# Numerators and denominators from one pass of 32x32 tiles, gathered by SBUF transfers

## The chip, the cores and the metric

The kernel runs on one core of a Trainium2 chip. The metric is the device time of one execution in microseconds (us). TensorE (PE) multiplies matrices and writes into PSUM; its weight loads are a row of their own in the profile (PEld). VectorE (DVE) and ScalarE (ACT) read and write PSUM and SBUF, GpSimd (POOL) here works on SBUF, and SyncE (SP) issues most DMA transfers. Each engine works through its own queue in order and waits where a semaphore says so.

## The reference

The input x has 16 images of 256 channels and 28x28 pixels. After a group norm, two layers follow that replace a 3x3 convolution by a lookup. Each channel has 16 centroids of 9 values. A pixel's 3x3 patch in a channel is compared with the channel's centroids, a softmax over the 16 distances gives weights, and the weights select rows of a table:

```python
d = sum(p*p) - 2*einsum('bncs,cks->bnck', p, centroids) + sum(centroids*centroids)
attn = softmax(-d, axis=-1)
lut = einsum('cks,cso->cko', centroids, w_sub)
out = einsum('bnck,cko->bno', attn, lut)
```

Batch norm and relu follow layer 1; batch norm, a squeeze-and-excite gate, two residual additions and a relu follow layer 2. The kernel never forms `lut`. It forms, per channel and pixel, the softmax-weighted centroid (9 numerators over one denominator) and multiplies this by `w_sub`. All data are float32.

## The kernel before

**Blocks.** An image of one layer is worked in four blocks: `hh` is the half of the 256 channels, `t` the upper or lower 14 rows, N = 14 x 28 = 392 pixels. There are 2 x 16 x 4 = 128 blocks (`blocks`, in the order `BLOCKS`). A block goes through these steps.

1. `patches` loads two tiles `pt` with the shifted rows of 128 channels from a copy in DRAM: 12 DMAs per block on SP.
2. `logits` (L622) multiplies them with the centroids in four passes, `mm` = 0 to 3. A pass is 16 matmuls with weights of 32x32; they fill the 16 squares of the array, and each streams 392 columns. In the profile every float32 matmul shows as two, so a pass is 32 records. A pass fills two tiles of two PSUM banks.
3. `exps` turns the logits into exponentials `e` in SBUF with two ACT instructions a pass. In layer 2 the pass `mm` = 0 of the blocks with `hh` = 0 goes through `wide_copy` to `wide_exp` instead (ACT, DVE, POOL, DVE, ACT), which subtracts the largest of the 16 logits first.
4. `num_a` (L673) multiplies `e` with eight of the nine centroid values: 8 matmuls of 64x32 per `mm`. `num_b` (L686) multiplies it with the ninth and with ones: 16 matmuls of 128x32 in one group. The ninth numerators and the denominators come out in different rows of one pair of banks. `split_r`, `join_r`, `split_q` and `join_q` (two on ACT, two on DVE) sort them into a tile `r` of denominators and a tile `qo` of ninth numerators.
5. `recip_dve` inverts `r`. `spread` copies it with stream shuffles to the rows where each numerator stands (`rb`, on DVE). `scale_a` multiplies the numerators by it on the way out of PSUM, on DVE. One or two pairs per block go another way: `copy_a` on ACT takes them out of PSUM, and `scale_q` on POOL multiplies them, as it does `qo`.

**Products.** The four blocks of an image are multiplied with the halves of `w_sub` by a scheme that needs seven products in place of eight (`PRODUCTS`: A11, S1, S3, S2, S4, A12, A22). Between them `mix` subtracts one block's tiles from another's, on POOL, in place (four times five instructions per image). A product is nine *stacks*: for each of nine k, two matmuls of 128x64 weights over 392 columns, accumulated in one bank. `acc_copy` (ACT) and `acc_add` (DVE) take the results out, and `reg_add` (POOL) adds two regions.

**Order.** The order of all work is written out by hand: `at(cluster, sub, function, ...)` puts a call at a place of a grid, and the calls are issued in the order of their places. There are two clusters per block. A product is one run of nine stacks behind one pass, except that S1 is split into seven and two. Which banks a step takes is set by `ROLES` and, for the first blocks, by `EARLY`; the ring has four tags of two banks. Numerators live in 12 tiles `qp` of two k each and 4 tiles `qo`.

**Around it.** While an image of layer 1 is worked, the next image's group norm is computed, written to DRAM (`to_home1`), and the finished image is written to DRAM for layer 2 (`to_home2`, an indirect DMA issued by POOL). While an image of layer 2 is worked, the previous one is gated, added and stored (`finish_...`, `store`). Some steps during layer 1 sort the codes and weights of layer 2 (`prep_...`, `sums_...`).

## Time and profile before

| | |
|---|---|
| median of 3 runs | 2579.1 us (2579.03 to 2579.27) |
| the profiled execution | 2580.25 us |
| its span, first to last instruction | 2578.8 us |
| granted TensorE clock | 1.000 |
| busy: PE, DVE, ACT, POOL | 99%, 69%, 53%, 74% of the span |
| moved by DMA | 372.09 MB |

A group row of the profile reads: line, engine, operation, output <- inputs, shapes, how many; then busy time in us, mean ns of one, idle time of the engine just before them and what ended it. A row of the order in time reads: start, duration, engine, line, operation. Layer 1 covers roughly the first half of the span. A long PE run between two weight-load rows can be read from their starts, since every matmul group begins with its loads.

### The profile page before, as it was taken

How to read it: one execution, taken by the hardware profiler on the slowest of the kernel's cores; microseconds unless marked ns; L12 is line 12 of the kernel's file. 1: busy time of each engine (PE TensorE's matmuls, PEld its weight loads, DVE VectorE, ACT ScalarE, POOL GpSimd, SP SyncE). 2: the span in 40 equal slices, each digit the busy share in tenths (PEclk: the TensorE clock that was granted, in tenths of full speed). 3: DMA queues.
4: the chain of work that ended last, by engine and by line, in shares of the span. 5: the costliest groups of instructions: out<-in, count | busy, mean ns of one | idle time of the engine just before them, and what ended most of it. 6: DMA issues, size and time to landing. Idle time of an engine off the chain costs nothing.

```text
span 2578.8 us, 85941 instructions
## 1 busy us (share of the span) xinstructions
PE 2561.5 (99%) x37082; PEld 1027.1 (40%) x37082; DVE 1776.3 (69%) x3797; ACT 1372.6 (53%) x1913; POOL 1911.6 (74%) x1346
## 2 busy tenths in 40 slices
PE   8999999999999999999999999999999999999998
PEld 3343334433343333433334334344444344433434
DVE  8766656666667666566676767767776667767676
ACT  6444444444444445444455655555655655555665
POOL 7686666776668776667676887878878788787786
PEclk9999999999999999999999999999999999999999
DMA  7556656565545575664664444444445444444442
GB/s 234 167 130 184 199 169 189 161 170 172 164 143 148 158 197 174 169 173 134 178 171 104 109 115 128 120 120 122 104 126 129 119 117 113 118 125 130 118 106 66
DMA packets 213289, 372.09 MB, mean 144 GB/s; under 512 B 29496, under 2 KB 183528, under 8 KB 212328
## 3 DMA queue, kind: packets, MB, share of 16 engines
q1 hardware_dynamic: 206584, 333.75, 48.2%
q0 software_dynamic: 6176, 32.66, 3.5%
q8 instruction: 296, 4.85, 0.8%
q14 instruction: 89, 0.73, 0.1%
q10 hardware_dynamic: 144, 0.10, 0.0%
HBM read 288.46 MB, written 77.95 MB: 142 GB/s over the span
## 4 chain that ended last, share of the span: by engine, by line
PE 96%; POOL 1%; DVE 1%; ACT 1%; DMA 1%; issue 0%; SPq 0%; POOLq 0%; DVEq 0%; ACTq 0%
PE acc L756 51%; PE lg L622 17%; PE na L673 14%; PE nb L686 13%; POOL qp L765 0%; ACT e L633 0%; DMA pt<-home 0%; ACT pt L1143 0%; POOL qp L736 0%; DVE qp L747 0%; DMA xt<-in_x 0%; POOL qo L763 0%; DMA d_sc<-score_t 0%; SPq L600 0%; PE sep L1049 0%
## 5 line engine op out<-in xcount | busy, mean ns | idle before, releaser
L756 PE MATMUL acc<-qp,wall 128*64 128x392 f32 x6176 | 1088.1, 494 | 1.0 <-POOL qp L765 0.4
L633 ACT ACTIVATE e<-lg 128x784 f32<-128x784 f32 x960 | 738.1, 821 | 624.7 <-PE lg L622 622.8
L765 POOL TENSOR_TENSOR qp<-qp,qp 128x784 f32<-128x784 f32 x512 | 946.3, 1872 | 146.2 <-DVE qp L747 145.7
L756 PEld LDWEIGHTS acc<-qp,wall 128*64 128x64 f32 x6176 | 424.3, 137 | 626.4 <-issue 529.8
L728 DVE STREAM_SHUFFLE rb<-r 128x392 f32<-128x392 f32 x1024 | 553.6, 608 | 0.0
L622 PE MATMUL lg<-pt,wd 32*32 32x392 f32 x15872 | 469.0, 499 | 0.6 <-DMA pt<-home 0.3
L699 DVE SCALAR_TENSOR_TENSOR r<-nb,kst,r 128x392 f32<-128x392 f32 x128 | 80.0, 625 | 432.7 <-ACT r L695 428.7
L673 PE MATMUL na<-e,cwa 64*32 64x392 f32 x8192 | 374.2, 492 | 0.0
L747 DVE TENSOR_TENSOR qp<-na,rb 128x784 f32<-128x784 f32 x352 | 333.9, 972 | 57.7 <-PE na L673 45.2
L686 PE MATMUL nb<-e,cwb 128*32 128x392 f32 x4096 | 366.3, 495 | 0.2 <-ACT e L633 0.2
L736 POOL TENSOR_TENSOR qo<-qo,rb 128x392 f32<-128x392 f32 x128 | 132.9, 1038 | 283.9 <-DVE rb L724 283.9
L713 DVE RECIPROCAL r<-r 128x392 f32<-128x392 f32 x128 | 333.2, 2603 | 4.4
L736 POOL TENSOR_TENSOR qp<-qp,rb 128x784 f32<-128x784 f32 x160 | 296.7, 1864 | 2.8
L673 PEld LDWEIGHTS na<-e,cwa 64*32 64x32 f32 x8192 | 182.4, 106 | 182.9 <-issue 73.0
L622 PEld LDWEIGHTS lg<-pt,wd 32*32 32x32 f32 x15872 | 116.1, 103 | 277.0 <-issue 235.6
L686 PEld LDWEIGHTS nb<-e,cwb 128*32 128x32 f32 x4096 | 135.0, 109 | 222.9 <-issue 155.0
L756 PE MATMUL acc<-qp,w_A 128*64 128x392 f32 x1024 | 181.1, 495 | 0.0
L695 ACT ACTIVATE r<-nb,kst 128x392 f32<-128x392 f32 x128 | 86.8, 678 | 154.9 <-PE nb L686 151.8
L756 PE MATMUL acc<-qo,wall 128*64 128x392 f32 (+1 forms) x772 | 159.2, 491 | 0.0
L657 POOL TENSOR_TENSOR z<-z,mx 128x1568 f32<-128x1568 f32 x32 | 91.9, 2872 | 86.1 <-DVE mx L651 84.8
L741 ACT COPY qp<-na 128x784 f32<-128x784 f32 x160 | 130.1, 813 | 21.6 <-PE na L673 20.1
L763 POOL TENSOR_TENSOR qo<-qo,qo 128x392 f32<-128x392 f32 x128 | 131.6, 1028 | 0.1
(244 smaller groups left out, 1624.4 us busy)
## 6 DMA issues: line engine op xcount, KB each, us to landing
pt<-home SPq DMA_DIRECT2D x744, 209.0 KB
pt<-home SPq DMA_DIRECT2D x744, 104.5 KB
home<-xpad SPq DMA_DIRECT2D x30, 899.0 KB
xt<-in_x SPq DMA_DIRECT2D x30, 784.0 KB
out_dram<-y SPq DMA_DIRECT2D x31, 392.0 KB
pt<-in_p SPq DMA_DIRECT2D x6, 784.0 KB
d_wS<-st SPq DMA_DIRECT2D x12, 192.0 KB
wall<-d_wS SPq DMA_DIRECT2D x4, 576.0 KB
```

The source lines that it names most:

```text
L622: nc.tensor.matmul(bk[32 * c : 32 * c + 32, :N].rearrange("p (r w) -> p r w", w=W), lhsT=(wx[u["hh"]] if early(u) else wts["wd", u["hh"]]) ...
L633: nc.scalar.activation(eg[:, 2 * i : 2 * i + 2, :], bk[:, :, :N], AF.Exp, scale=2.0)
L673: nc.tensor.matmul(bs[32 * i : 32 * i + 32, r, :N], lhsT=wts["cwa", u["hh"]][64 * r : 64 * r + 64, mm, i, :], rhs=es[64 * r : 64 * r + 64, ...
L686: nc.tensor.matmul(bs[32 * i : 32 * i + 32, mm >> 1, :N], lhsT=wts["cwb", u["hh"]][:, mm, i, :], rhs=es[:, i, :], start=mm % 2 == 0, stop= ...
L713: nc.vector.reciprocal(u["r"], u["r"])
L728: nc.vector.stream_shuffle(rb[:, r, :], u["r"], mask_of(2 * mm + r))
L736: nc.gpsimd.tensor_tensor(q, q, u.pop(("rb", mm)), ALU.mult)
L741: nc.scalar.copy(pair(u, mm), u.pop(("na", mm))[:, :, :N])
L747: nc.vector.tensor_mul(pair(u, mm), u.pop(("na", mm))[:, :, :N], rb)
L756: nc.tensor.matmul(accs[key][o : o + AW, : cols[1] - cols[0]], lhsT=wl[w][:, k, o : o + AW], rhs=us["q", k][:, cols[0] : cols[1]], start=f ...
L763: nc.gpsimd.tensor_tensor(out_u["q", 8], in0["q", 8], in1["q", 8], ALU.subtract)
L765: nc.gpsimd.tensor_tensor(pair(out_u, mm), pair(in0, mm), pair(in1, mm), ALU.subtract)
```

## The change

Steps 4 and 5 and the order are replaced.

- `codes` takes the place of `num_a` and `num_b`: per `mm` one pass of 16 matmuls with weights of 32x32, like `logits`, gives the eight numerators, the ninth numerator and the denominator of 64 channels together, in two tiles of two banks (`cd`).
- `take` copies each `cd` to SBUF with two instructions on ACT (in block 0 one of them on DVE). For `mm` 1 and 3 the copy goes into a tile `qq` of four k; for `mm` 2 and 0 it goes into a tile `g`.
- `moves` issues DMAs from SBUF to SBUF on SP: for each `mm` one of 32 rows of 392 numbers into the denominators `sum` and one into the ninth numerators `qo`, and for `mm` 2 and 0 one more of 64 rows of 1568 numbers from `g` into the other rows of `qq`. That is ten per block.
- `recip` sums `sum` (for a later test) and inverts it on DVE. `spread` is as before, without the shuffle for the ninth numerator. `scale` multiplies in SBUF: three pairs per block on DVE, one pair and the ninth numerator on POOL.
- Every pass, `logits` or `codes`, is followed by two stacks: the order is now counted in positions, eight to a block and 32 to an image, and the stacks of the seven products are laid out evenly over the positions.
- PSUM is three rotating tags of two banks for passes and two single banks for products.
- The preparation of layer 2's codes gives one array `cn` in place of `cwa` and `cwb`, and the weights are loaded by two DMAs with every second row in place of one. At the end `gate_wide` and `finish_wide` are gone, and the image before the last is finished by `finish_fast`.

```diff
-NQ = {"pair": 12, "one": 4}
+NQ = {"quad": 9, "one": 5}
+PRODUCTS = (("A11", 0), ("S1", 0), ("S4", 2), ("S3", 1), ("S2", 0), ("A12", 3), ("A22", 0))
+NPOS = {1: 5, 2: 7, 3: 9, 0: 11}
+IMG, START = 32, 24
+HEAD = ((18, 24), (25, 31), (32, 37.7))
...
+    def banks(name, tag=None):
+        if tag is None:
+            spin[0] = (spin[0] + 1) % 3
+            tag = spin[0] - 1 if spin[0] else 2
+        return p_ring.tile([P, 2, 512], F32, tag=f"t{tag}", name=name)
...
+    def codes(u, mm):
+        bs = [banks("cd") for _ in range(2)]
+        es = u.pop(("e", mm))
+        for c in range(4):
+            for i in range(4):
                 nc.tensor.matmul(
+                    bs[c // 2][32 * i : 32 * i + 32, c % 2, :N],
+                    lhsT=wts["cn", u["hh"]][32 * c : 32 * c + 32, mm, i, :], rhs=es[32 * c : 32 * c + 32, i, :],
                     start=True, stop=True,
                 )
...
+    def take(u, mm, engines):
+        x, guest = divmod(turn_of(mm), 2)
+        t = epool.tile([P, 4, N], F32, tag="g", name="g", bufs=2) if guest else quad(u, x)
+        for n, bk in enumerate(u.pop(("cd", mm))):
+            if engines[n] is nc.scalar:
+                nc.scalar.copy(t[:, 2 * n : 2 * n + 2, :], bk[:, :, :N])
...
+    def moves(u, mm, eng=None):
+        eng = eng or nc.sync
+        turn, t = turn_of(mm), u.pop(("cd", mm))
+        guest = turn & 1
+        for off, dst in ((1 - guest, u["s"]), (3 - guest, lone(u))):
+            eng.dma_start(dst[turn::4, :], t[off::16])
+        if guest:
+            eng.dma_start(quad(u, turn >> 1)[1::2], t[1::2])
+
+    def recip(u):
+        w = u["w"]
+        nc.vector.tensor_reduce(wsum[:, w : w + 1], u["s"], axis=AX.X, op=ALU.add)
+        nc.vector.reciprocal(u["s"], u["s"])
...
+    def scale(u, x, eng):
+        if x == 4:
+            eng.tensor_tensor(lone(u), lone(u), u["s"], ALU.mult)
         else:
+            eng.tensor_tensor(pair(u, x), pair(u, x), u.pop(("rb", x)), ALU.mult)
...
+        for mm in range(4):
+            at(g + 2 * mm, logits, u, mm)
...
+            s = g + NPOS[mm]
+            at(s, codes, u, mm)
+            at(s + 0.1, take, u, mm, (nc.scalar, nc.vector if j == 0 else nc.scalar))
+            at(s + 0.12, moves, u, mm)
+        s = g + 13.2
+        at(s, recip, u)
+        at(s + 1.3, scale, u, 4, nc.gpsimd)
+        for i, d in enumerate(SPREADS):
+            at(s + 1.35 + 0.9 * i, spread, u, d)
+            at(s + 1.4 + 0.9 * i, scale, u, d, nc.gpsimd if d == 3 else nc.vector)
...
+            for k in range(NS):
+                pos = x0 + (x1 - x0) * (k + 0.5) / NS
+                pos = int(pos) + 0.2 + 0.75 * (pos - int(pos))
+                at(pos, product, (n, w), us[r], w, (k,), k == 0, k == NS - 1, ps=q % 2)
```

## The prediction

> **What bounds the kernel now.** I read the page's sums and its chain of waits first, then the busy time by stretches of both layers, then TensorE's weight loads in order of time, because their starts show what each segment of the PE queue costs.

> ```profile
> span 2578.8 us, 85941 instructions
> PE 2561.5 (99%) x37082; PEld 1027.1 (40%) x37082; DVE 1776.3 (69%) x3797; ACT 1372.6 (53%) x1913; POOL 1911.6 (74%) x1346
> PE 96%; POOL 1%; DVE 1%; ACT 1%; DMA 1%; issue 0%; SPq 0%; POOLq 0%; DVEq 0%; ACTq 0%
> q1 hardware_dynamic: 206584, 333.75, 48.2%
> ```
> ```profile
> 1300.00:2500.00 1200.00, 1199.95 (x17428) 480.19 (x17428) 854.70 (x1688) 697.20 (x967) 946.30 (x573) 1.00 0.46 120
> 400.00:1200.00 800.00, 799.20 (x11642) 317.81 (x11628) 515.82 (x1189) 381.62 (x524) 557.17 (x436) 1.00 0.59 167
> 13.00:40.00 27.00, 25.33 (x466) 10.47 (x468) 22.38 (x61) 17.46 (x25) 22.82 (x34) 1.00 0.83 281
> ```
> The columns of the stretches are PE, PEld, DVE, ACT, POOL busy, granted clock, DMA share, GB/s. PE is busy without a gap in both layers at clock 1.00 and carries 96% of the chain: time is what the PE queue holds, and other engines cost nothing until PE waits for them. The weight loads tell what it holds:

> ```profile
> 1010.09 0.17 PEld L686 LDWEIGHTS nb<-e,cwb 128*32 128x32 f32 x8 [0.64 <-ACT hpad L787]
> ...
> 1012.88 0.23 PEld L622 LDWEIGHTS lg<-pt,wd 32*32 32x32 f32 x32 [0.64 <-issue]
> ...
> 1018.51 0.23 PEld L622 LDWEIGHTS lg<-pt,wd 32*32 32x32 f32 x32 [0.61 <-PE acc L756]
> 1019.38 1.55 PEld L673 LDWEIGHTS na<-e,cwa 64*32 64x32 f32 x48 [0.64 <-issue]
> ...
> 1022.23 0.23 PEld L622 LDWEIGHTS lg<-pt,wd 32*32 32x32 f32 x32 [0.64 <-issue]
> 1023.10 0.20 PEld L756 LDWEIGHTS acc<-qp,wall 128*64 128x64 f32 x4 [0.64 <-issue]
> 1024.57 0.23 PEld L622 LDWEIGHTS lg<-pt,wd 32*32 32x32 f32 x32 [0.61 <-DVE rb L724]
> ...
> 1029.48 0.20 PEld L756 LDWEIGHTS acc<-qp,wall 128*64 128x64 f32 x4 [0.64 <-issue]
> 1035.56 0.23 PEld L622 LDWEIGHTS lg<-pt,wd 32*32 32x32 f32 x32 [0.61 <-issue]
> ```
> Start to next start: a logits pass 0.87 us (1018.51 to 1019.38), na of a block 2.85 (1019.38 to 1022.23), nb 2.79 (1010.09 to 1012.88), a run of two product stacks 1.47 (1023.10 to 1024.57), of nine 6.08 (1029.48 to 1035.56). So a stack is (6.08 - 1.47) / 7 = 0.659 and the change of tile shape adds 1.47 - 2 x 0.659 = 0.15 to a run. An image of one layer is 16 x 0.87 + 4 x 5.64 + 63 x 0.659 + 8 x 0.15 = 79.2; 32 of them are 2534 of the span, and the other 45 are small products, head and tail.

> **The change, term 1: the passes.** Per block na and nb (5.64) go and four passes cd come. cd has lg's tile, 32*32, sixteen matmuls and 392 columns, and stands between stacks as lg does: 0.87, so 3.48. 128 x (3.48 - 5.64) = -276.

> **Term 2: the runs.** The 63 stacks of an image stood in 8 runs (S1 was split); now they stand in 32, two behind each pass. 24 x 0.15 x 32 = +117. Terms 1 and 2: -159, an image of 74.2. A pass and its two stacks, 0.87 + 1.47 = 2.34, are one position of the new order, 32 to an image. [...]

> **Term 3: ScalarE and the PSUM banks.** Each pass, logits and cd alike, must now be copied out by ACT, through three rotating bank pairs.

> ```profile
> 1013.88 1.54 ACT L633 ACTIVATE e<-lg 128x784 f32<-128x784 f32 x2 [0.19 <-PE lg L622]
> ```
> ```profile
> L741 ACT COPY qp<-na 128x784 f32<-128x784 f32 x160 | 130.1, 813 | 21.6 <-PE na L673 20.1
> L705 ACT ACTIVATE qo<-nb,kst 128x392 f32<-128x392 f32 x128 | 87.4, 683 | 0.7 <-DVE r L699 0.7
> L695 ACT ACTIVATE r<-nb,kst 128x392 f32<-128x392 f32 x128 | 86.8, 678 | 154.9 <-PE nb L686 151.8 <-issue 3.1
> L807 ACT ACTIVATE hpad<-hpad,bnsh,bnsc 128x392 f32<-128x392 f32 x64 | 44.2, 719 | 59.8 <-DVE hpad L793 51.8 <-DVE gn_var L570 8.0
> L820 ACT ACTIVATE y<-y,bnsh,bnsc 128x784 f32<-128x784 f32 x30 | 31.0, 1034 | 0.0
> L579 ACT ACTIVATE xpad<-xt,nrm 128x784 f32<-128x784 f32 x30 | 29.7, 1047 | 0.3 <-POOL nrm L573 0.3
> L665 ACT ACTIVATE e<-e 128x1568 f32<-128x1568 f32 x32 | 48.4, 1511 | 72.9 <-DVE e L661 72.9
> ```
> By the stretches ACT has 381.62 / 800 x 79.2 = 37.8 an image in layer 1 and 46.0 in layer 2. Minus the splits (4 x 1.36) and copies (4 or 6 x 0.81), plus 16 x 1.54: 53.7 and 60.3 of 74.2, enough in sum. But a pass at T is taken up from T + 1.00 (1012.88, 1013.88), its first half is free at about T + 1.8, and the pass after next half needs it at T + 2.34, one position later: slack about 0.5. Every other ACT job of 0.7 to 1.5 us makes ACT late; at 1.54 of 2.34 it recovers 0.8 per position. The order puts two to four such jobs on neighbouring positions (layer 1: L807 and L579 near positions 17 to 20; layer 2: gate, norm_both, xn near 18 to 22, and again near 25). I reckon the excess over 0.5 as 1.2 us an image in layer 1 and 2.1 in layer 2: +53. The ends are 0 and all ACT work beside the 32 x 1.54 = 49.3 uncovered, 4.4 and 11.0 an image: 16 x 15.4 = 246. I take a fifth, nearer the lower end, since most of these jobs stand alone on their position and 0.5 + 0.8 swallows them.

> **Term 4: VectorE and GpSimd.** DVE loses the joins, one shuffle and the product out of PSUM, and gets a sum (half of 949) and three products per block with both inputs in SBUF.

> ```profile
> L747 DVE TENSOR_TENSOR qp<-na,rb 128x784 f32<-128x784 f32 x352 | 333.9, 972 | 57.7 <-PE na L673 45.2 <-issue 2.9 <-POOL z L657 0.5
> L699 DVE SCALAR_TENSOR_TENSOR r<-nb,kst,r 128x392 f32<-128x392 f32 x128 | 80.0, 625 | 432.7 <-ACT r L695 428.7
> L724 DVE STREAM_SHUFFLE rb<-r 128x392 f32<-128x392 f32 x128 | 76.6, 598 | 0.0
> L710 DVE SCALAR_TENSOR_TENSOR qo<-nb,kst,qo 128x392 f32<-128x392 f32 x128 | 67.5, 527 | 0.0
> L1131 DVE TENSOR_REDUCE qsum<-qp 128x2 f32<-128x784 f32 x4 | 3.7, 949 | 0.0
> L736 POOL TENSOR_TENSOR qo<-qo,rb 128x392 f32<-128x392 f32 x128 | 132.9, 1038 | 283.9 <-DVE rb L724 283.9
> L736 POOL TENSOR_TENSOR qp<-qp,rb 128x784 f32<-128x784 f32 x160 | 296.7, 1864 | 2.8
> ```
> ```profile
> 67.31 2.73 DVE L239 TENSOR_TENSOR wall<-w_A,wall 128x1152 f32<-128x1152 f32 x1
> ```
> ```profile
> 63.30 5.52 POOL L765 TENSOR_TENSOR qp<-qp,qp 128x784 f32<-128x784 f32 x3 [0.60 <-DVE qp L747]
> 68.78 2.16 POOL L736 TENSOR_TENSOR qo<-qo,rb 128x392 f32<-128x392 f32 x1
> ```
> The one DVE product of two SBUF tensors here waits for POOL's running mix to end at 68.8, and POOL's next takes 2.16 for 1.04: they exclude each other. For 784 columns POOL loses 1.12 x 784 / 1152 = 0.76; DVE takes 0.95 alone and up to 0.95 + 1.86 behind a POOL product, taken 1.6. [...] Per image DVE comes to 51.1 - 19.0 + 1.9 + 12 x 1.6 = 53.2 in layer 1 and 56.4 - 17.0 + 21.1 = 60.5 in layer 2; POOL, with two scales less in layer 2, to 55.2 + 9.1 = 64 and 62.5 - 3.7 + 9.1 = 68. All below 74.2, so nothing in sum; their queues are in order, and late mixes cost the products, which have 1 to 3 positions in hand: +12, with ends 0 and 100.

> **Term 5: the transfers.** Ten more per block on SP, about 1.2 MB.

> ```profile
> L600 SPq DMA_DIRECT2D pt<-home x1488: 543/587/1449, 56.7 to 2515.5; - x186
> DMA to landing us min/median/max: 3.3/5.2/8.3
> ```
> The first row is the time on SP's queue (min, median, max, ns), the second the landing of transfers on the tile home. SP: 22 x 0.587 = 12.9 of 18.6 us per block. Transfers: 154 MB at q1's 48.2% for 333.75 MB is 22 points, 18 us an image; in the shorter image the shares are (0.59 x 79.2 + 18) / 74.2 = 0.87 and 0.73. The moves wait for the copies, and behind them on SP stand the patch loads, whose last issue has about 4 positions, 9.4 us, against a worst landing of 8.3: covered, barely. The sums must land before DVE's reciprocal, 2.2 positions after the last cd: 5.1 - 1.00 - 1.54 - 0.59 = 2.0 us. At 3.3 DVE stands 1.3 a block, with its shuffles, accumulator adds and the turns of the wide blocks behind it: 53 + 5 and 61 + 5 an image, still under 74. Costed in term 4. The preparation of layer 2's codes and weights changes its layout and some transfers; PE's full queue hides it as it does now: 0.

> **Head and tail.** Until position 18 there is no product, and ACT sets the pace: 9 logits and 3 cd at 1.54 and four half cd, 21.6, against 16 x 0.87 + 3 of raw sums on PE. Before, PE was busy 25.33 of 27. +10 (0 to 20). The tail keeps its chain: 0, give or take 5.

> **Sum.** -159 + 53 + 12 + 10 = -84. The profiled execution took 2580.25 us (span 2578.8), 1.15 over the median 2579.1: 2495.

> **Rivals.** *All is hidden*: terms 1, 2 and half the head, 2425. For it: ACT, DVE, POOL all under 74.2. Against: a slack of 0.5. Chance 0.15. *POOL and DVE hold each other up*: POOL's 68 plus the 283.9 / 32 = 8.9 it now idles for DVE gives 77 an image in layer 2, 16 x 2.8 = 45, and half of that loss in layer 1, 22; with the banks and the head 2579 - 159 + 67 + 53 + 10 = 2550. Chance 0.15. *The sums land late, and it is slower*: at 8.3 (the worst row) DVE stands 6.3 a block, and its mean image is 56.9 + 25.2 = 82.1, over 79.2: 2579 + 32 x 2.9 = 2672. It decides from 56.9 + 4 w = 79.2, w = 5.6, a landing of 7.6. For it: the DMA share of 0.87 in layer 1 and patch loads just ahead in the queue; against: 50 KB pieces. Chance 0.18.

> **How the numbers follow.** My forecast, 2445 to 2545, has 0.50; the remaining 0.02 is no change within 0.2%, about what a measurement of this kernel can tell. Faster 0.80, same 0.02, slower 0.18. The range takes in the rivals' bodies, 2422 to 2600: about 0.07 lies below and 0.12 above.

> **What would show it.** Starts of weight loads: cd 0.87, two stacks 1.47. PE busy about 2420 and idle where it waits for ACT (term 3) rather than for qq (term 4). DVE products of 1.0 to 2.8 us, mixes lengthened by 0.8. Sums landing near 3 us. It is wrong if cd costs more than lg, or if DVE's wait for the sum exceeds 5 us.

## The result, and the profile after

The changed kernel takes 2986.2 us (median of 4 runs, 2981.98 to 2993.31), the kernel before 2579.1: a ratio of 1.158, 95% interval 1.156 to 1.161. It is slower by 407 us, where 84 us less were forecast. The profiled execution took 2993.3 us. First the page of the changed kernel and two stretches, with the columns of the prediction's stretches:

```profile
span 2991.8 us, 97156 instructions
PE 2640.3 (88%) x41178; PEld 800.0 (27%) x41178; DVE 1929.2 (64%) x3290; ACT 1845.2 (62%) x2533; POOL 2000.4 (67%) x1293
...
L697 DVE TENSOR_TENSOR qq<-qq,rb 128x784 f32<-128x784 f32 x384 | 623.5, 1624 | 28.4 <-ACT g L662 0.9
L713 POOL TENSOR_TENSOR qq<-qq,qq 128x784 f32<-128x784 f32 x510 | 1041.5, 2061 | 28.3 <-DVE qq L697 19.8
L678 DVE TENSOR_REDUCE wsum<-sum 128x1 f32<-128x392 f32 x128 | 70.6, 552 | 766.9 <-DMA sum<-g 655.6
```
```profile
400.00:1200.00 800.00, 717.27 (x11352) 214.20 (x11338) 475.61 (x902) 475.76 (x638) 516.19 (x366) 0.94 0.71 201
1300.00:2500.00 1200.00, 1076.90 (x16958) 321.96 (x16954) 817.56 (x1277) 771.54 (x1056) 840.32 (x479) 0.95 0.61 165
```
No engine is full. PE, which had no gap before, is busy for 0.90 of both stretches, and its granted clock is 0.94 and 0.95. Some waits of the changed kernel (total us, how often, longest):

```profile
PE cd L641 <- ACT e L599: 87.0, 39, 7.2
PE acc L706 <- DVE qq L697: 76.3, 47, 3.0
PE acc L706 <- POOL qq L713: 76.0, 23, 5.5
DVE wsum L678 <- DMA sum<-g: 655.6, 89, 18.2
```
PE waits about equally for exponentials, for scaled numerators and for mixes. Only VectorE's wait for the denominators stands out, and it doesn't stop PE by itself. The row has the waits that the profile puts down to `sum<-g`; with the few that it puts down to another transfer they are the 766.9 us of the page, and this total is meant by VectorE's wait from here on. How it arises is seen in rows picked from the order in time:

```profile
1503.03 1.54 PE L706 MATMUL acc<-qq,wall 128*64 128x392 f32 x8
1503.77 4.53 SPq L567 DMA_DIRECT2D pt<-home  x6
1504.50 0.94 PE L641 MATMUL cd<-e,cn 32*32 32x392 f32 x32
1505.37 0.88 PE L706 MATMUL acc<-qo,wall 128*64 128x392 f32 x4
1505.54 1.53 ACT L662 COPY g<-cd 128x784 f32<-128x784 f32 x2 [0.18 <-ACT hpad L755]
1506.83 0.94 PE L585 MATMUL lg<-pt,wd 32*32 32x392 f32 x32
1508.40 0.63 SPq L672 DMA_DIRECT2D sum<-g  x1
1512.45 0.56 DVE L678 TENSOR_REDUCE wsum<-sum 128x1 f32<-128x392 f32 x1 [5.59 <-DMA sum<-g]
```
The pass costs what was forecast, start to next start: cd 0.87 (1504.50 to 1505.37), two stacks 1.47 (1503.03 to 1504.50). The copy of its results ends at 1507.07. SyncE is then still issuing six patch loads, the last denominators go out at 1508.40, and VectorE can use them at 1512.45, 4.05 us later, having stood for 5.59.

When such a delay reaches PE, more follows. Another place of the changed kernel, and its stretches of 2 us:

```profile
1895.47 0.56 DVE L678 TENSOR_REDUCE wsum<-sum 128x1 f32<-128x392 f32 x1 [14.26 <-DMA sum<-g]
1899.99 0.98 DVE L697 TENSOR_TENSOR qq<-qq,rb 128x784 f32<-128x784 f32 x1
1901.03 2.52 PE L706 MATMUL acc<-qq,wall 128*64 128x392 f32 x8 [2.45 <-DVE qq L697]
```
```profile
1902.00:1904.00 2.00, 2.00 (x22) 0.52 (x34) 1.90 (x4) 0.00 (x0) 1.94 (x2) 0.50 0.98 181
1904.00:1906.00 2.00, 2.00 (x38) 0.63 (x8) 2.00 (x2) 0.86 (x2) 2.00 (x1) 0.79 0.83 284
```
PE waits 2.45 us for the product behind the late denominators. From 1901.44 its clock is halved for 3.41 us: PE is busy, but the eight matmuls at 1901.03 take 2.52 us, where those at 1503.03 took 1.54. Over rows of 1 us from 40 us to the end, PE is idle for 343 us (8 before), and busy time times (1 - clock) sums to 147 us (0 before).

### The profile page after: what moved, and what is told of

Same layout as the page of the kernel before. It is cut to its first block, busy times and chain, and to the rows that moved or that the text cites. A ratio compares the mean times of both kernels' runs of the same rounds, so it can differ in the third digit from the quotient of the medians.

```text
span 2991.8 us, 97156 instructions
## 1 busy us (share of the span) xinstructions
PE 2640.3 (88%) x41178; PEld 800.0 (27%) x41178; DVE 1929.2 (64%) x3290; ACT 1845.2 (62%) x2533; POOL 2000.4 (67%) x1293
## 5 line engine op out<-in xcount | busy, mean ns | idle before, releaser
L706 PE MATMUL acc<-qq,wall 128*64 128x392 f32 x6176 | 1286.3, 530 | 153.0 <-DVE qq L697 76.3
L713 POOL TENSOR_TENSOR qq<-qq,qq 128x784 f32<-128x784 f32 x510 | 1041.5, 2061 | 28.3 <-DVE qq L697 19.8
L706 PEld LDWEIGHTS acc<-qq,wall 128*64 128x64 f32 x6176 | 391.4, 142 | 972.8 <-issue 670.4
L641 PE MATMUL cd<-e,cn 32*32 32x392 f32 x16384 | 568.0, 518 | 87.3 <-ACT e L599 87.0
L697 DVE TENSOR_TENSOR qq<-qq,rb 128x784 f32<-128x784 f32 x384 | 623.5, 1624 | 28.4 <-ACT g L662 0.9
L678 DVE TENSOR_REDUCE wsum<-sum 128x1 f32<-128x392 f32 x128 | 70.6, 552 | 766.9 <-DMA sum<-g 655.6
L690 DVE STREAM_SHUFFLE rb<-sum 128x392 f32<-128x392 f32 x1024 | 556.8, 602 | 1.0 <-issue 0.4
L662 ACT COPY g<-cd 128x784 f32<-128x784 f32 x510 | 391.2, 816 | 180.7 <-issue 66.8
L662 ACT COPY qq<-cd 128x784 f32<-128x784 f32 x510 | 389.1, 815 | 170.2 <-PE cd L641 155.8
L695 POOL TENSOR_TENSOR qo<-qo,sum 128x392 f32<-128x392 f32 x128 | 143.2, 1119 | 414.3 <-DVE sum L679 316.5
L697 POOL TENSOR_TENSOR qq<-qq,rb 128x784 f32<-128x784 f32 x128 | 252.7, 1974 | 147.7 <-DVE rb L690 65.7
L679 DVE RECIPROCAL sum<-sum 128x392 f32<-128x392 f32 x128 | 333.2, 2603 | 4.4
L776 POOL DMA_INDIRECT home<-hpad,col x60 | 62.5, 1042 | 208.5 <-DMA home<-hpad,col 66.6
```

The source lines that it names most:

```text
L641: nc.tensor.matmul(bs[c // 2][32 * i : 32 * i + 32, c % 2, :N], lhsT=wts["cn", u["hh"]][32 * c : 32 * c + 32, mm, i, :], rhs=es[32 * c : 3 ...
L662: nc.scalar.copy(t[:, 2 * n : 2 * n + 2, :], bk[:, :, :N])
L678: nc.vector.tensor_reduce(wsum[:, w : w + 1], u["s"], axis=AX.X, op=ALU.add)
L679: nc.vector.reciprocal(u["s"], u["s"])
L690: nc.vector.stream_shuffle(rb[:, r, :], u["s"], mask_of(2 * x + r))
L695: eng.tensor_tensor(lone(u), lone(u), u["s"], ALU.mult)
```

## The experiments

Each time is that of one execution; the kernel before took 2577.4 to 2579.4 us beside them. Differences are to 2986 us where nothing else is named. The changed kernel's own runs lie 11 us apart, so less than some 15 us is not read. Five theories: L, the denominators land late; B, ScalarE and the three bank pairs bound the passes; P, products of two SBUF operands on VectorE and products on GpSimd shut each other out (labels and expectations call this the port; what the two share, no run shows); S, GpSimd stands at its own scatters; C, a gap on PE halves its clock for a while.

### The transfers left out

`e1_no_sums` issues no transfer of denominators (they are ones, the exponentials are of zero).
```diff
...
-        for off, dst in ((1 - guest, u["s"]), (3 - guest, lone(u))):
+        for off, dst in ((3 - guest, lone(u)),):
```

> The changed kernel without the eight-row gathers of the denominators: sum holds ones, so the division is left out, and the exponentials are taken with scale 0 to keep the numbers finite (same instructions and shapes). The ninth numerators and the guest rows are still gathered. Theory L (VectorE stands in order for the denominators' transfer, 767 us in all, and what is queued behind it starves PE): time falls from 2986 to about 2560, the waits of wsum vanish, PE's granted clock returns to 0.98 or more. Theory B (ScalarE and the three bank pairs bound the passes): 2900 or more, since nothing on ScalarE changes. Theory P (VectorE and GpSimd exclude each other at the products out of SBUF): 2850 or more, since no product changes.

`e2_no_moves` makes `moves` empty, with ones in `sum` and `qo`.

> The changed kernel with none of the ten transfers per block: sum and qo hold ones, the rows of qq that were gathered keep what the copy left there, exponentials with scale 0. Division and the gathered numerators are left out. Theory L: as without the denominators' gathers, or lower by up to 80 us if the other eight transfers' place on SP's queue and the DMA engines count too; what then stands above 2425 is terms 3 and 4 of the prediction. Theory B: still 2850 or more. Theory P: still 2800 or more.

2767.2 and 2722.2 us. B expected 2900 or more and falls. L expected about 2560 and a clock of 0.98, and doesn't hold alone: the clock is 0.95 and 0.955. The denominators are worth 219 of 264 us, and 300 above the forecast with all hidden (2425) are left without any transfer. The profile of e2_no_moves shows what is still wrong there, in VectorE's and GpSimd's order of time:

```profile
999.77 11.50 DVE L693 TENSOR_TENSOR qq<-qq,rb 128x784 f32<-128x784 f32 x1
```
```profile
999.39 3.65 POOL L709 TENSOR_TENSOR qq<-qq,qq 128x784 f32<-128x784 f32 x2
1003.00 1.02 POOL L709 TENSOR_TENSOR qo<-qo,qo 128x392 f32<-128x392 f32 x1
1003.98 1.02 POOL L691 TENSOR_TENSOR qo<-qo,sum 128x392 f32<-128x392 f32 x1
1004.96 1.86 POOL L693 TENSOR_TENSOR qq<-qq,rb 128x784 f32<-128x784 f32 x1
1006.77 3.66 POOL L709 TENSOR_TENSOR qq<-qq,qq 128x784 f32<-128x784 f32 x2
1011.42 3.69 POOL L709 TENSOR_TENSOR qq<-qq,qq 128x784 f32<-128x784 f32 x2 [0.99 <-DVE qq L693]
```
GpSimd runs seven products back to back from 999.39 to 1010.43, and a product on VectorE that takes 0.98 in the median ends only in the first pause, after 11.50 us. GpSimd's pause, 0.99 us, is itself a wait for this product. In the changed kernel the longest product of VectorE took 4.70 us.

### Products of two SBUF operands on VectorE

`p1_no_port`: VectorE's three products per block become shuffles that read one SBUF operand.
```diff
-            eng.tensor_tensor(pair(u, x), pair(u, x), u.pop(("rb", x)), ALU.mult)
...
+            for r in range(2):
+                eng.stream_shuffle(q[:, r, :], rb[:, r, :], list(range(32)))
```

> Edit: the changed kernel, but VectorE's three products per block of numerators by reciprocals (two inputs in SBUF) become pairs of shuffles that write the spread reciprocals over the numerators (one input in SBUF); the numerators are so lost and the exponentials are of zero. Theory P (VectorE's products of two SBUF operands and GpSimd's products shut each other out): GpSimd's mixes fall from 2.06 us back to 1.87, no shuffle is over 0.7 us, PE's waits for mixes (76 us) fall under 25, and the time comes to 2690 to 2780. Theory L (the denominators' transfer alone sets the loss, with the clock behind each gap): VectorE still waits 5 to 6 us a block for the sums, and the time stays over 2880.

> Edit: both at once: no transfer of numerators or denominators (as in e2_no_moves) and no product of two SBUF operands on VectorE (as in p1_no_port). If the late transfers (L) and the shared port (P) are the whole of the loss, PE's idle time falls under 50 us, the mean clock is over 0.99 and the time is 2420 to 2480, the forecast with all hidden. If a third cause is left (the wide path, the banks), the time stays over 2560, with PE's wait for the exponentials near the 50 us of e2_no_moves.

2803.7 and 2629.3 us. GpSimd's mixes are back at 1.87 us. The first time lies between its two expectations, and PE's wait for mixes falls only from 76 to 62 us, not under 25. P is worth 182 us with the transfers in and 93 without them (2722.2 to 2629.3); the transfers 174 us without P. But 2629 is more than L and P alone would leave, and the wide path isn't the rest: PE waits 9 us for exponentials. GpSimd's order of time in the second shows a third cause:

```profile
627.75 1.08 POOL L777 DMA_INDIRECT home<-hpad,col  x1 [2.79 <-ACT hpad L756]
637.11 0.97 POOL L777 DMA_INDIRECT home<-hpad,col  x1 [8.28 <-DMA home<-hpad,col]
645.79 1.01 POOL L777 DMA_INDIRECT home<-hpad,col  x1 [4.84 <-DMA home<-hpad,col]
646.82 1.87 POOL L714 TENSOR_TENSOR qq<-qq,qq 128x784 f32<-128x784 f32 x1
```
A scatter of layer 1's output waits until the one before has landed, 8.28 us, because the new order has the two one position apart. In all GpSimd waits 128 us for scatters to land, in the kernel before 34. The next image's mixes stand behind them.

### The scatters

`h1_spaced` in the changed kernel, `p3_rest` on p2_no_port_no_moves:
```diff
-                        at(ends[5 + o] + 1.3 + r, to_home2, b, o, r)
+                        at(ends[5] + 1.3 + 4.2 * (2 * o + r), to_home2, b, o, r)
```

> Edit: the changed kernel, but layer 1's four scatters of an image (GpSimd's indirect transfers of the finished sums) stand 4.2 positions (9.8 us) apart in the order in place of 1 position. Theory S (GpSimd stands behind its own scatter, each of which waits until the one before has landed, and the next image's mixes stand behind it): GpSimd's waits at the scatters, 208 us, fall under 90, layer 1's images (88 to 99 us each) fall by 4 to 8 us, layer 2's stay at 92, and the time is 2870 to 2940. Theories L and P alone: layer 1 is late for the sums and the port as layer 2 is, GpSimd's waits at the scatters are slack, and the time stays within 2960 to 3010.

> Edit: three at once: no transfers of numerators and denominators, no product of two SBUF operands on VectorE (both as in p2_no_port_no_moves), and the scatters spaced as in h1_spaced. If S is the whole of what was left in p2_no_port_no_moves: layer 1's images come down from 84 to 86 us to the 76.5 of layer 2 there, and the time is 2480 to 2540. If not, layer 1 stays over 80 us an image and the time over 2570.

2976.2 us: no more than the spread, though GpSimd's wait at the scatters fell from 208 us to 9. There GpSimd now stands longer for the denominators, ahead of the product that makes `qo` (528 us, 414 before the edit). And p3_rest takes 2534.8 us: 94 less than p2_no_port_no_moves. So S costs 94 us where the other causes are gone, and nothing that can be read while they are there. A stretch of p3_rest, and an event of consecutive images, first two of layer 1, then two of layer 2:

```profile
1300.00:2500.00 1200.00, 1177.04 (x19660) 366.98 (x19660) 851.88 (x2074) 918.59 (x1287) 917.34 (x555) 0.99 0.46 120
```
```profile
881.77 0.23 PE L509 MATMUL gnp<-gn_dv,gmat 128*64 128x2 f32 x4
956.92 0.23 PE L509 MATMUL gnp<-gn_dv,gmat 128*64 128x2 f32 x4
1713.53 0.23 PE L509 MATMUL sep<-se_hh,w_sb 128*64 128x2 f32 x4
1790.00 0.23 PE L509 MATMUL sep<-se_hh,w_sb 128*64 128x2 f32 x4
```
The same event in layer 2 of the kernel before:

```profile
1840.26 0.23 PE L540 MATMUL sep<-se_hh,w_sb 128*64 128x2 f32 x4
1919.65 0.23 PE L540 MATMUL sep<-se_hh,w_sb 128*64 128x2 f32 x4
```
PE is nearly full again, and an undisturbed image takes 75.2 us in layer 1 and 76.5 in layer 2, in the kernel before 79.4. Most of what layer 2's image has over the forecast's 74.2 is seen in a pass of it:

```profile
1730.13 0.90 PE L643 MATMUL cd<-e,cn 32*32 32x392 f32 x16
1731.25 0.90 PE L643 MATMUL cd<-e,cn 32*32 32x392 f32 x16 [0.22 <-ACT e L601]
1732.07 1.54 PE L707 MATMUL acc<-qq,wall 128*64 128x392 f32 x8
```
The second half waits for ScalarE's exponentials, and the pass takes 1.94 us from start to next start in place of 0.87, though only 0.22 are recorded as PE's idle time. Outside half-clock stretches all passes of p3_rest together are late by 45 us in this way: 1.0 us an image in layer 1, 2.1 in layer 2. In 37 of 44 us of the longer delays the weight loads inside the pass wait for ScalarE.

`q3_moves` is p1_no_port with the scatters spaced.

> Edit: p1_no_port with the scatters spaced as in h1_spaced: all ten transfers are in, the products of two SBUF operands on VectorE and the scatters' waits are out. Its distance to p3_rest (2535) is what the transfers alone cost. If causes add: p1_no_port less 50 to 95, 2710 to 2755, so 175 to 220 for the transfers. If the transfers hide the scatters as in h1_spaced (17 us): 2780 to 2800, so some 250 for the transfers.

2806.8 us, no gain over p1_no_port (2803.7). The transfers alone therefore cost 2806.8 - 2534.8 = 272 us, the largest of the three.

### What makes the denominators late

`o1_order` issues the patch loads a quarter of a position later: behind a pass's moves, not ahead of them.
```diff
-                at(g - 5.1 + 4 * p, patches, u, p)
+                at(g - 4.85 + 4 * p, patches, u, p)
```

> Edit: the changed kernel, but SyncE issues each six patch loads 0.25 position later in the order, so that they stand behind the moves of a pass (the last denominators of a block among them) and not ahead of them. Theory L, in the form that SyncE's order makes the denominators late: from the end of the copy to the issue the last denominators take 0.7 to 1.5 us in place of a mean of 2.5, VectorE's wait falls from 767 us to 500 to 650, and the time to 2880 to 2960. Rival: SyncE now stands for the copies with the patch loads behind it, PE waits for patches (12.8 us now) over 60 us, and the time is 2980 to 3080.

2896.8 us, 89 less. VectorE's wait falls from 767 to 526 us. Over the blocks in which VectorE waits, the last denominators were issued 2.60 us after their copy (mean) and are now issued after 0.76; from issue to use they took 4.74 us (median) and now take 2.34, with no patch loads in front of them. But its waits read:

```profile
PE lg L585 <- DMA pt<-home: 194.3, 98, 14.9
DVE wsum L678 <- DMA sum<-g: 464.9, 82, 22.3
PE acc L706 <- POOL qq L713: 7.7, 4, 5.3
```
PE's waits for numerators and mixes are all but gone, and in their place it waits for patch loads, which stand behind moves that wait for copies.

`q1_sums_only` leaves out the six transfers that carry no denominators.

> Edit: the changed kernel with 4 of its 10 transfers a block: the four of the denominators; those of the last numerators and the pairs are left out (the exponentials are of zero). If SyncE's queue is the fault (10 issues of 0.6 us a block beside 12 patch loads, the denominators and the patch loads in each other's way): VectorE's wait for the sums falls under 500 us, most of the 271 us that all ten cost comes back, and the time is 2770 to 2870. If it is the length of the chain from pass to reciprocal alone (copy, one transfer, landing): the wait stays over 650 us and the time over 2930.

2903.4 us. The time lies between the two expectations; VectorE's wait stays at 654 us, as the second has it. Six issues less bring 83 us, and the four transfers of denominators and their chain carry the rest, 181 us (to e2_no_moves). How these 181 divide between the chain's length and the patch loads ahead of it no run shows.

`e3_act_sum`: ScalarE issues the block's last denominators.
```diff
-            eng.dma_start(dst[turn::4, :], t[off::16])
+            (nc.scalar if mm == 0 and dst is u["s"] and eng is nc.sync else eng).dma_start(dst[turn::4, :], t[off::16])
```

> The changed kernel, all of its work, with one transfer per block moved: the last gather of denominators (mm 0) is issued by ScalarE right behind its copies and no longer by SP behind patch loads and stores. Theory L with the delay on SP's queue: VectorE's wait for the denominators falls from 767 to 350 or less and the time to about 2750, less some 40 us that ScalarE pays for 128 issues. If the delay is in the DMA engines themselves (landing 4.7 us whoever issues), the wait stays above 650 and the time at 2950 to 3000. Theories B and P: 2986 or more.

3056.2 us, 70 more. VectorE's wait fell to 541 us, but PE waits 214 us for patch loads (13 before the edit). SyncE's own waits tell where these became late:

```profile
SPq L567 <- DMA sum<-g: 295.8, 56, 7.2
```
Over all lines SyncE stands 731 us until a transfer of denominators has landed, by the releasers that the profile infers, and 0.6 in the changed kernel. For one, an issue at 1513.08 waited 6.16 us for the transfer that ScalarE had issued at 1510.94, and six patch loads stood behind it. So the edit moved the wait onto the queue that it was to relieve; why an issue of SyncE has to wait for ScalarE's transfer stays open.

`f1_late`: the reciprocals 1.5 positions later.
```diff
-        s = g + 13.2
+        s = g + (13.2 if j < 4 else 14.7)
```

> Edit: the changed kernel, but the reciprocals and all that follows them in the block come 1.5 positions (3.5 us) later, from the fifth block on. L: VectorE's wait for the sums falls from 767 us to 300 to 450, and the time to 2850 to 2920. P: the products then come later against the same mixes and product stacks, GpSimd and VectorE meet as often as before, PE's waits for numerators and mixes grow, and the time is 2970 to 3080.

2919.5 us, 67 less. VectorE's wait is 607 us, above the 300 to 450 that L had; PE's wait for scaled numerators grew from 76 to 150. In both kernels every one of these waits is for products of an image's third block: its stacks follow its reciprocals soonest, and with the later reciprocals they come later still.

### The wide path

`w1_sub_dve`: `wide_sub` on VectorE.
```diff
-        nc.gpsimd.tensor_tensor(zk, zk, mx.unsqueeze(2).to_broadcast([P, N // 4, K]), ALU.subtract)
+        nc.vector.tensor_tensor(zk, zk, mx.unsqueeze(2).to_broadcast([P, N // 4, K]), ALU.subtract)
```

> Edit: the changed kernel, but the wide path's subtraction of the maxima (32 of 2.87 us) runs on VectorE in place of GpSimd. If the wide path waits because the subtraction stands behind mixes in GpSimd's order: PE's wait for exponentials falls from 87 to under 40 us and the time to 2870 to 2930. If VectorE's subtraction, with two SBUF inputs, is itself shut out while GpSimd runs products back to back (P): its mean is over 3 us, and the time is 2960 to 3050.

2943.8 us, 42 less, between the expectations: PE's wait for exponentials falls from 87 to 51 us. The subtraction takes 1.85 us (mean) and was never shut out for long, 1.93 at most. Of the 32, 16 met no product of GpSimd; the other 16 began some 0.27 us before the end of one, ran next, and the product of GpSimd behind them took 3.42 us in place of 1.87. So these 16 got their turn between two products of GpSimd; the product of 11.50 us in e2_no_moves didn't.

### The clock

`c1_stalls` and `c2_gaps` put gaps into the kernel before. In c1_stalls a small product, a ScalarE copy that depends on it and a small product that waits for the copy make a gap, one per image in layer 1 and four in a row in layer 2. In c2_gaps there is one gap per image, made longer by more copies (4 in layer 1, 8 in layer 2); its line is:
```diff
+                at(g + 5, 2.1, stall, g + 5, 3 + 4 * l)
```

> The kernel before, with TensorE made to wait once per image at one place, for the images 1 to 15 of layer 1 by one exchange with ScalarE (a small product, a copy out of PSUM, a product of the copy) and for the images of layer 2 but the last by four such exchanges. It measures what a gap on TensorE costs beside itself. If a gap costs only its length, the time rises by the sum of the idle PE time, some 15 x 1 + 15 x 4 = 75 us, and the granted clock stays 1.00. If a gap of some length halves the clock for some us behind it, the clock falls below 1.00 and the time rises by 30 to 60 us more than the idle PE time, in layer 2 above all.

> Edit: the kernel before, with one artificial gap on PE in the images 2 to 31: a small product, copies of one tile on ScalarE that depend on it (4 in layer 1, 8 in layer 2), a small product that waits for them. Theory C (a gap on PE of some 3 us halves the clock that is granted for some 5 us after it, a short one does not): after layer 2's gaps of 3 us or more rows of 2 us show a clock near 0.5, after layer 1's shorter ones near 1.0; the mean clock is 0.97 to 0.99 and the time 2660 to 2720. Rival (the clock falls for another reason than the gap): the clock stays over 0.99 and the time is 2620 to 2660.

2647.2 and 2721.1 us. In c1_stalls (gaps of at most 0.6 us) the mean clock is 0.994: no single gap halved it, 5 of the 15 rows of four did. c2_gaps has 15 gaps of 1.91 us and 15 of 4.11. Three of its gaps, and the stretches behind the second and third:

```profile
543.52 0.23 PE L540 MATMUL stl<-stl,gmat 128*64 128x2 f32 x2 [1.91 <-ACT stl L775]
707.05 0.23 PE L540 MATMUL stl<-stl,gmat 128*64 128x2 f32 x2 [1.91 <-ACT stl L775]
1724.38 0.27 PE L540 MATMUL stl<-stl,gmat 128*64 128x2 f32 x2 [4.11 <-ACT stl L775]
```
```profile
543.00:545.00 2.00, 1.34 (x40) 0.63 (x44) 0.00 (x0) 0.93 (x3) 2.00 (x2) 1.00 0.16 65
707.00:709.00 2.00, 1.79 (x13) 0.56 (x14) 0.00 (x0) 0.38 (x1) 2.00 (x2) 0.55 0.00 0
709.00:711.00 2.00, 2.00 (x41) 0.54 (x44) 0.56 (x1) 0.37 (x1) 2.00 (x3) 0.59 0.00 0
1725.00:1727.00 2.00, 2.00 (x40) 0.28 (x16) 0.00 (x0) 0.61 (x1) 1.22 (x1) 0.50 0.04 8
1727.00:1729.00 2.00, 2.00 (x24) 0.70 (x20) 0.00 (x0) 0.93 (x2) 0.00 (x0) 0.80 0.00 0
```
The clock was halved at all 15 long gaps and at 5 of the 15 short ones; 1 - clock sums to 1.7 us at nearly every one, so 3.4 us at half. The gaps make the slow clock, in a kernel that has no other change: its mean clock is 0.985, that of the kernel before beside it 0.999. The clock records of the trace add when it is halved: all 22 half-clock stretches of c2_gaps begin on one grid of 3.413 us, within 4 ns, wherever their gap lies, and so do all 65 of the changed kernel, of which 26 last 3.413 us and 33 last 6.827. Four of the five short gaps that halved the clock lie whole between two lines of this grid, and only one of the ten that didn't. Why the grid is there no run shows.

### Versions with nothing left out

`v1_psum`: VectorE's shuffles write the spread reciprocals into the idle bank of the product stacks, and its products read one operand there.
```diff
+    def spread_scale(u, x, r, pos):
+        q, rb = pair(u, x)[:, r, :], bank("rp", idle_bank(pos))[:, :N]
+        nc.vector.stream_shuffle(rb, u["s"], mask_of(2 * x + r))
+        nc.vector.tensor_mul(q, q, rb)
```

> Edit: the changed kernel with nothing left out, but from the second image on VectorE's shuffles write the spread reciprocals into the PSUM bank of the product stacks that is idle, and its products (6 of 392 columns in place of 3 of 784 per block) read one operand from there. P: with one operand in PSUM VectorE and GpSimd no longer shut each other out, GpSimd's mixes are back at 1.87 us, and the gain is that of p1_no_port: 2780 to 2850. Against it: the product stacks now wait for VectorE to hand the bank back, or the products are shut out all the same; then 2930 or more.

2983.0 us, no gain. A group and two waits of it:

```profile
L702 DVE TENSOR_TENSOR qq<-qq,rp 128x392 f32<-128x392 f32 x744 | 418.2, 562 | 36.0 <-ACT g L662 0.5 <-DMA pt<-home 0.4 <-ACT qq L662 0.4
PE acc L711 <- DVE qq L702: 137.4, 82, 7.0
PE sep L1003 <- DVE qq L702: 111.0, 15, 9.6
```
With one operand in PSUM all 744 products take 0.56 us (0.561 to 0.567): P is confirmed a second way. But as VectorE is late for the denominators, the bank comes back late, and PE waits 248 us for these products.

`v2_all` adds h1_spaced and f1_late, with a block's spreads closer together. `v3a` adds o1_order, has the reciprocals 1 position later in place of 1.5, starts the stacks one position later, and has a tenth buffer `qq`. `v3b` has GpSimd issue layer 2's stores.

> Edit: v1_psum, h1_spaced and f1_late together, with nothing left out. If P, S and the late sums are separate causes, their gains add (about 190 + 70 + 75): 2640 to 2720. If each uncovers the next one's wait as soon as it is gone: 2750 or more. Faster than the kernel before (2579) only if the clock's share (147 us in the changed kernel) goes with the gaps.

> Edit, nothing left out: as v2_all (reciprocals spread into the idle PSUM bank, scatters spaced, reciprocals 1 position later), with the patch loads behind the moves as in o1_order, all product stacks one position (2.34 us) later, and a tenth buffer of numerators in the space of two buffers of spread reciprocals. If the third block's chain (copy, transfer, reciprocal, spread, product) against its first stack, which had no slack, was what PE still waited for in v2_all (218 us): under 100 us, and the time 2620 to 2750. If not: 2850 or more. To be faster than the kernel before, PE's idle time has to fall under 100 us in all.

> Edit, nothing left out: v3a, with layer 2's stores issued by GpSimd in place of SyncE, which waits for GpSimd's last sums ahead of the patch loads and moves behind them. If stores still hold the denominators back: 20 to 60 us under v3a. If not: v3a plus 0 to 30, the issues on GpSimd.

2914.4, 2861.0 and 2863.2 us. v3a is the best version that computes everything, and still 282 us slower than the kernel before. PE's wait for scaled numerators fell from 218 us in v2_all to 33, as v3a's first expectation has it, but not the time: the wait for patch loads is 118, the largest that is left, out of 305 us of idle PE. The stores make no difference.

## Why the prediction was wrong

**Terms 1 and 2 (passes and runs, -159).** They held: 0.87 for a pass, and 1.47 for two stacks. In p3_rest an undisturbed image takes 75.2 and 76.5 us in place of 74.2; of the 1.0 and 2.3 between, 0.2 and 0.3 are small products and 0.7 and 2.0 the late passes of term 3.

**Term 3 (ScalarE and banks, +53).** It held, in kind and nearly in size, as far as p3_rest shows, where ScalarE has the same work: 1.0 and 2.1 us an image for the 1.2 and 2.1 forecast, some 50 us in 32 images. The fifth that I took between the ends was a guess, so the size is partly luck. PE's recorded wait for exponentials there, 8.4 us, doesn't show it, since the delay lies inside passes.

**Term 4 (VectorE and GpSimd, +12, ends 0 and 100).** It failed at "all below 74.2, so nothing in sum". The product's duration was right (1.62 for the 1.6 taken), the mixes lengthened by only 0.19 us, not 0.76, and both engines stayed under 70%; it cost 93 to 182 us all the same. I let a product on VectorE wait for one product of GpSimd; it took up to 4.70 us in the changed kernel, and without the transfers one waited for seven. And sums of busy time don't tell whether work is there when PE needs it. The rival in which the two hold each other up had the mechanism, at 67 us.

**Term 5 (transfers, 0) is the step that failed most: 272 us.** "Covered, barely" held neither way. I had SyncE's time as 12.9 of 18.6 us and looked for what stands behind the moves; I didn't see what stands ahead of the last denominators: six patch loads, 0.22 position earlier in the order, 3.7 us of issues in the median and 4.53 in the row shown. The sums took 4.74 us from issue to use, not 3.3, after a mean of 2.60 for SyncE. VectorE stood 767 / 128 = 6.0 us a block, not 1.3, which is over the 5 us that the prediction named as its sign of being wrong. The rival in which the sums land late named this wait, and its threshold of 5.6 was passed; but its 2672 was priced by VectorE's sum alone, and VectorE, 64% busy and 26% standing for denominators, still wasn't full. The cost came by another way, to PE: all 76 us of its waits for VectorE's products are for the third block of an image, and 70 of the 76 for mixes are for the first two mixes of S1, on GpSimd, whose order stands for the same reciprocals.

**Not in the prediction: the scatters.** I went through what is added, not through what the new order brings closer together: 94 us once the other causes are gone.

**Not in the prediction: the clock.** Every wait was priced at its length. From p3_rest to the changed kernel PE's idle time grows by 343 - 57 = 286 us and the slow clock's loss by 147 - 19 = 128, of 459 in the span. Most of the other 45 lie inside passes, as in term 3: outside half-clock stretches, lateness that isn't recorded as idle time is 67 us in the changed kernel and 39 in p3_rest.

**The account.** With three causes out the time is 2534.8, 40 over the forecast: PE is still idle for 57 us (8 before) and loses 19 to the slow clock, and no cause of the size of a hundred us is left. The gains do not add, since one wait covers another: P is worth 182 or 93, the transfers 174, 264 or 272, the scatters nothing or 94, by what else is there.

## What to carry to other kernels

When PE's queue is full, a change that shortens it and leaves every other engine below 75% can still lose (here 407 us, with VectorE, ScalarE and GpSimd at 64, 62 and 67%): follow the longest chain from a pass to the first use of its result through each queue, in the order of issue, and see which instructions stand directly ahead of the one that is waited for. Price a gap on PE at its length plus what a halved clock takes: in c2_gaps some 1.7 us behind each of the 15 gaps of 4.11 us and behind 5 of the 15 of 1.91, and in c1_stalls 5 of the 15 rows of four gaps of at most 0.6 us halved it too. Read a segment's cost from start to next start: the pass of p3_rest that took 1.94 us for 0.87 has only 0.22 recorded as idle time. Remove suspected causes together as well as one by one; here one taken out alone (the scatters) showed nothing.
